# Layer 0's input rows added in its second loop, layer 2's outputs loaded into buffers of their own, and the v rows stored tile by tile

## The chip, the cores and the metric

The kernel runs on one core of a Trainium2 chip. The core has five engines with an instruction queue each: TensorE (PE, matrix products and transposes into the accumulation memory PSUM), VectorE (DVE), ScalarE (ACT), GpSimd (POOL) and SyncE (SP), which only issues DMAs. ScalarE and GpSimd issue DMAs as well, in the order of their own queues. Each queue is worked off in order, and an instruction waits in it for the semaphores of what it needs. The metric is the time on the device in microseconds (us), as the median of the timed runs; lower is better.

## The reference: four graph layers with residuals

The input x has 2708 rows of 512 features, and adj is a symmetric 2708 x 2708 matrix of zeros and ones. Each layer computes `x = layernorm(x + layer(x, adj))`. Cut to what matters here:

```python
# layer 0: the first 64 neighbours of each row
keep = Ab & (cumsum(Ab, axis=1) <= 64)
cnt  = keep.sum(axis=1)
xj = leaky_relu((keep @ x / max(cnt, 1)) @ W_nb.T + b_nb)
xi = leaky_relu(x @ W_line.T + b_line)
x  = layernorm(x + xi + where(cnt > 0, xj, 0))
# layer 1
agg = mask @ x / max(deg, 1)
x  = layernorm(x + relu(concat(x @ W_self + b_self, agg @ W_nb + b_nb) @ W_comb + b_comb))
# layer 2: attention with 8 heads of 64 features
e  = leaky_relu(f1[:, None] + f2[None, :], 0.2), masked by adj
x  = layernorm(x + softmax(e) @ Wh)
# layer 3: the same attention, elu, a second attention with one head, then an MLP 512-1024-512
x  = layernorm(x + MLP(elu(attention(elu(attention(x))))))
```

In layer 0 the layer norm therefore has three summands in each row: x itself, xi ("own rows"), and xj.

## The kernel before

Rows are handled in 22 tiles of 128 (the last has 20). What follows is only what the change touches; line numbers are those of the profile.

**Layer 0, first loop** (L297 to L324). For each tile TensorE transposes x and makes two products (L228): with W_nb (kept as a high and a low part, yH at L222 by ScalarE and yL at L223 by VectorE, which releases the accumulation tile), and with W_line. From the second product VectorE makes u = pm + b_line (L317), the leaky relu (`leaky`, L186) and adds the tile's x (L319); GpSimd stores u to `r0_dram` (L320). Between these, 14 of the tiles each have one block of rows of the adjacency mask prepared: ScalarE counts (L246), VectorE makes a running count in two halves (the scan L252 and the product L255), and TensorE transposes the mask (L264), which ScalarE writes to `maskT`. The second half of the running count is held behind the instruction named `low` on VectorE. Mask blocks are loaded by GpSimd (L241) into three buffers.

**Layer 0, second loop.** For blocks of up to four tiles TensorE accumulates the masked sums over all 22 column tiles (L460). The eight remaining mask blocks, the folding of layer 1's weights and the products for the attention vectors (L443, L444) go on beside it in small steps. When a block is summed, `finish` completes its tiles in steps that are taken one by one from the next block's loop: load r0, bias and leaky relu (L380, L186), a yield, then u * has + r0 (L383), the layer norm, and a store to `x1_dram`. The last block's steps fall into the loop that follows, layer 1's projection.

**Projections** (`project`, L568 to L681, called for layers 2, 3 and 4). For each tile: rows, transposed (L124, L126), 16 products (L627), small exponentials on ScalarE, and the scaled rows R2 (L656). Of each row's score b a factor v = exp(-0.8 b) is kept as a row (`keep_v`): TensorE transposes b (L604), ScalarE writes the exponential into `vrow` (L605), which is as wide as a block of the attention, and SyncE stores it to `v_dram` once for each block (L608). The attention loads v from there, spread over all partitions (L697, L712). For layers 2 and 3 the first such load is made at tile 14 (`first`).

**Layer 3's source** (`summed`, L929 to L938). A tile's attention output of layer 2 is loaded from `o_dram`, divided, x2 is added, and the layer norm is written over it; GpSimd stores it to `x3_dram` (L937), and TensorE transposes it. The tile comes from the ring "rows" of the pool `ahead`, three buffers, which r0, the rows of x and of x1 and others use too (`fetched`, L162 to L165). x2 comes into a ring of two buffers, "spare".

The order of the instructions in each queue is made by the framework's planner, from the order of the source, the dependences, the free buffers and its own estimates of durations. `issue_after` and `pe` add orders written by hand. A buffer is free again when the last instruction that uses its tile is done, a DMA included.

Of the kernel before, what the change touches and what calls it, by code (L numbers as in the profile page):

```python
# [9 lines left out]
F32 = mybir.dt.float32  # L10
# [3 lines left out]
AF = mybir.ActivationFunctionType  # L14
# [4 lines left out]
P = 128  # L19
D = 512  # L20
KD = D // P
EPS = 1e-5
ALPHA = 0.2
# [7 lines left out]
def kernel(  # L31
# [9 lines left out]
    nc = tc.nc  # L41
# [8 lines left out]
    def rows(t):  # L50
        return min(P, N - t * P)
# [31 lines left out]
    r0_dram = dram.tile([N, D], F32, name="r0_dram")  # L83
    x1_dram = dram.tile([N, D], F32, name="x1_dram")
    z1_dram = dram.tile([N, D], F32, name="z1_dram")
    x2_dram = dram.tile([N, D], F32, name="x2_dram")
    x3_dram = dram.tile([N, D], F32, name="x3_dram")


    o_dram = dram.tile([N, D], F32, name="o_dram")  # L90
# [15 lines left out]
    def layer_norm(pool, y, n, dst, on_scalar=False):  # L106
        st = pool.tile([P, 6], F32, name="ln_st")
        nc.vector.bn_stats(st[:n], y)
        mv = pool.tile([P, 2], F32, name="ln_mv")
        nc.vector.bn_aggr(mv[:n], st[:n])  # L110
        rs = pool.tile([P, 1], F32, name="ln_rs")
        nc.vector.tensor_scalar(rs[:n], mv[:n, 1:2], EPS, None, op0=OP.add)
        nc.gpsimd.tensor_tensor(rs[:n], rs[:n], half[:n], OP.pow)
        if not on_scalar:
            nc.vector.tensor_scalar(dst, y, mv[:n, 0:1], rs[:n], op0=OP.subtract, op1=OP.mult)
            return
        nc.vector.scalar_tensor_tensor(mv[:n, 0:1], mv[:n, 0:1], -1.0, rs[:n], op0=OP.mult, op1=OP.mult)
        nc.scalar.activation(dst, y, AF.Identity, bias=mv[:n, 0:1], scale=rs[:n])
# [22 lines left out]
    ahead = fast.enter_context(tc.tile_pool(name="ahead", bufs=2))  # L141
# [4 lines left out]
    def weight():  # L146
        return weight_tile().rearrange("p k a c -> p (k a c)")[:, :KD * D].rearrange("p (k c) -> p k c", k=KD)
# [14 lines left out]
    def fetched(src, t, n, pool=ahead, name="rows", bufs=None):  # L162
        x_ = pool.tile([P, D], F32, name=name, bufs=bufs or (3 if pool is ahead else None))
        nc.sync.dma_start(x_[:n], src[t * P:t * P + n, :])
        return x_[:n]  # L165
# [19 lines left out]
    def leaky(dst, u):  # L185
        return nc.vector.scalar_tensor_tensor(dst, u, 0.01, u, op0=OP.mult, op1=OP.max)  # L186
# [7 lines left out]
    with ExitStack() as phase:  # L194
# [17 lines left out]
        sm = phase.enter_context(tc.tile_pool(name="l01", bufs=2))  # L212
# [22 lines left out]
        cuts = [(b, min(b + 4, NT)) for b in range(0, NT, 4)]  # L235
        cuts = cuts[-1:] + cuts[:-1]
# [35 lines left out]
        def rows_of(src):  # L272
            return early(2, NT, lambda t: fetched(src, t, rows(t)))

        with ExitStack() as ph:
            st = ph.enter_context(tc.tile_pool(name="l0a", bufs=1))
            wnT, wlT = weight(), weight2
            room = [maskT[:, G + k, :4 * D].bitcast(F32) for k in range(2 * KD)]

            xs = rows_of(x)
            xTs = early(0, NT, lambda t, order=as_it_comes: transposed(ahead, ps_tr, xs(t), rows(t), "xT", order))

            transpose_weight(room[:KD], ps_tr, wnT, l0_w_nb)
            lows = {}
            for t in range(2):
                xT = xTs(t, order=pe)
                lows[t] = keep_y(t, P, product(xT, P, wnT, 0, pe))
            transpose_weight(room[KD:], ps_tr, wlT, l0_w_line)  # L290
            b_line = bias(bcast(l0_b_line, D))
            masks = early(1, HERE, lambda i: load_mask(i, st.tile([P, N], BF16, name="m", bufs=3)))
            masks(0)
            nc.gpsimd.memset(maskT[:, NT - 1, :], 0.0)
            nc.gpsimd.memset(maskT[:, :, N:], 0.0)
            counted = turned = 0
            for t in range(NT):  # L297
                n = rows(t)
                if t > 1:
                    lows[t] = keep_y(t, n, product(xTs(t, order=pe), n, wnT, 0, pe))  # L300
                xT = xTs(t)
                if t + 1 < NT:
                    xTs(t + 1, order=pe)
                while turned < counted - (t + 1 < NT):
                    for _ in turn(turned, masks(turned), lambda: sums(BF16, (P, G, P)), pe):
                        pass
                    turned += 1
                now = counted < min(HERE, -(-(t - 1) * HERE // (NT - 5)))
                if now:
                    m, places = masks(counted), st.tile([P, N // 2], BF16, name="places", bufs=1)  # L310
                    with tc.issue_after(highs[t].ins):
                        count(counted, m)
                    with tc.issue_after(lows[t].ins):
                        place(counted, m, places, 0, 2)
                pm = product(xT, n, wlT, 1, pe)
                u = sm.tile([P, D], F32, name="u")
                nc.vector.tensor_add(u[:n], pm[:n], b_line[:n])  # L317
                leaky(u[:n], u[:n])
                low = nc.vector.tensor_add(u[:n], u[:n], xs(t))  # L319
                nc.gpsimd.dma_start(r0_dram[t * P:t * P + n, :], u[:n])  # L320
                if now:
                    with tc.issue_after(low.ins):
                        place(counted, m, places, 1, 2)
                    counted += 1  # L324
# [3 lines left out]
        with ExitStack() as ph:  # L328
# [47 lines left out]
            def finish(ts_, us):  # L376
                for t in ts_:
                    n, u = rows(t), us[t]
                    r0 = fetched(r0_dram, t, n)
                    nc.vector.tensor_add(u[:n], u[:n], b_nb[:n])  # L380
                    leaky(u[:n], u[:n])
                    yield
                    nc.vector.scalar_tensor_tensor(u[:n], u[:n], has[:n, t:t + 1], r0, op0=OP.mult, op1=OP.add)  # L383
                    layer_norm(sm, u[:n], n, u[:n])
                    nc.gpsimd.dma_start(x1_dram[t * P:t * P + n, :], u[:n])
                    yield
# [63 lines left out]
            for i, b in enumerate(cuts):  # L450
# [19 lines left out]
                for t in ts_:  # L470
                    n = rows(t)
# [7 lines left out]
            xs = rows_of(x1_dram)  # L479
            xTs = early(0, NT, lambda t: transposed(ahead, ps_tr, xs(t), rows(t), "xT"))  # L480
            for t in range(NT):
                n = rows(t)
# [6 lines left out]
                u = sm.tile([P, D], F32, name="u")  # L489
# [3 lines left out]
        with ExitStack() as ph:  # L493
            st = ph.enter_context(tc.tile_pool(name="l1b", bufs=2))
            for t in range(NT):
                n = rows(t)
# [11 lines left out]
                u = sm.tile([P, D], F32, name="u")  # L508
# [5 lines left out]
    late = fast.enter_context(tc.tile_pool(name="late", bufs=1))  # L514
# [51 lines left out]
    def project(name, source, layer, v_dram, cuts, turned=None, first=None):  # L566


        w_src, w_view, _, heads = atts[layer]
# [9 lines left out]
        with ExitStack() as ph:  # L579
            sm = ph.enter_context(tc.tile_pool(name=f"{name}_s", bufs=2))  # L580
# [3 lines left out]
                           for k in (("pv", "pmm") if first else ("pmm", "pv")))  # L584
            if not first:
                ps_v, ps_mm = ps_mm, ps_v
            width = max(z - a for a, z in cuts) * P
            xs = early(1, NT, lambda t: source(sm, t, rows(t)))
            xTs = early(0, NT, lambda t: transposed(ahead, ps_tr, xs(t), rows(t), "xT"))
            if turned:  # L590
# [1 line left out]
                cuts_ = [(t, t + 1) for t in range(3)] + [(t, min(t + 2, NT)) for t in range(3, NT, 2)]  # L592
                parts = early(2, len(cuts_), lambda i: ready[i] if i in ready else turned(sm, *cuts_[i]))
                xTs = lambda t: parts(t if t < 3 else (t - 3) // 2 + 3)[:, :, ((t - 3) % 2 if t > 2 else 0) * P:][:, :, :P]
            vrows, bs, scaled = {}, {}, {}

            def keep_v(t):
                n = rows(t)
                a, z = next(c for c in cuts if c[0] <= t < c[1])
                if t == a:  # L600
                    vrows[a] = sm.tile([heads, width], F32, name="vrow", bufs=1)
                vrow = vrows[a]
                ps = ps_v.tile([P, P], F32, name="ps_v")
                nc.tensor.transpose(ps[:heads, :n], bs[t][:n, :heads], ident[:n, :n])  # L604
                nc.scalar.activation(vrow[:, (t - a) * P:(t - a) * P + n], ps[:heads, :n], AF.Exp, scale=ALPHA - 1.0)  # L605
                if t == z - 1:
                    cols = slice(a * P, a * P + (z - 1 - a) * P + n)
                    nc.sync.dma_start(v_dram[:, cols], vrow[:, :cols.stop - cols.start])  # L608

            for t in range(NT):  # L610
                n = rows(t)
# [53 lines left out]
                a, z = next(c for c in cuts if c[0] <= t < c[1])  # L665
# [68 lines left out]
    cuts = [-((-NT * i) // nb) for i in range(nb + 1)]  # L734
# [193 lines left out]

    def summed(sm, t, n):  # L929

        o, x2 = fetched(o_dram, t, n), fetched(x2_dram, t, n, late, "spare", 2)
        b = next(i for i, (a, z) in enumerate(blocks) if a <= t < z)
        by_head = o.rearrange("p (h c) -> p h c", h=H)
        nc.vector.tensor_mul(by_head, by_head, rcs[:n, b, :, t - blocks[b][0], None].to_broadcast([n, H, HO]))
        nc.vector.tensor_add(o, o, x2)
        layer_norm(late, o, n, o, on_scalar=True)
        nc.gpsimd.dma_start(x3_dram[t * P:t * P + n, :], o)  # L937
        return o  # L938

    loads, ready = [], {}  # L940

# [157 lines left out]
    scaled = project("p4", None, 2, vd[2], quads, elu_turned)  # L1099
# [327 lines left out]
```

## Time and profile before

| what | us |
|---|---|
| median of 3 timed runs | 2994.57 |
| lowest and highest of them | 2991.03, 2997.17 |
| the profiled execution | 2990.11 |
| its span, first to last instruction | 2988.3 |

Stretches of the span, with the busy time of the engines in each:

| stretch, us | work | TensorE | VectorE | ScalarE |
|---|---|---|---|---|
| 0 to 216 | layer 0, first loop | 189.25 | 166.47 | 93.07 |
| 216 to 506 | layer 0, second loop | 281.98 | 171.69 | 143.17 |
| 506 to 665 | layer 1, projection | 156.98 | 66.80 | 23.83 |
| 665 to 885 | layer 1, neighbour sums | 220.00 | 64.47 | 62.53 |
| 885 to 977 | layer 2, projection | 90.48 | 37.35 | 42.88 |
| 977 to 1523 | layer 2, attention | 533.53 | 536.26 | 506.49 |
| 1523 to 1640 | layer 3, projection | 104.05 | 77.16 | 62.60 |
| 1640 to 2185 | layer 3, first attention | 528.02 | 536.47 | 500.49 |
| 2185 to 2268 | layer 3, second projection | 80.52 | 36.72 | 38.65 |
| 2268 to 2988 | second attention and MLP | 702.62 | 304.49 | 60.02 |

The stretches are cut where one kind of product ends and the next begins; neighbouring stages overlap a little. An engine is busy while an instruction runs on it; DMA issues and waits don't count. Products are pipelined, so that a busy TensorE is not one at its peak. TensorE's granted clock was 0.995 of full speed over the span. In the page's lists "L164 rows<-o_dram" means that line 164 writes the tile rows from the tensor o_dram; numbers at the end of names are left out, so that x1_dram, x2_dram and x3_dram all read x_dram.

### The profile page before, as it was taken

What the parts mean: (1) busy time and instruction counts of PE and PEld (TensorE: products, weight loads), DVE (VectorE), ACT (ScalarE), POOL (GpSimd) and SP (SyncE); (2) the same over time, 40 slices, a digit from 0 to 9 for tenths busy, and PEclk for the clock granted to TensorE, in tenths of its full rate; (3) what the DMA queues carried; (4) which work ended last, traced back from release to release, by engine and by line L of the source; (5) the groups of instructions that cost most, each with busy time, mean ns of one, the idle gap of its engine ahead of it and who ended that gap; (6) DMA issues with size and microseconds to landing.
All of it is one profiled execution on the core that took longest, in us unless ns stands there. A gap on an engine that the chain in (4) does not pass through costs nothing.

```text
span 2988.3 us, 36484 instructions
## 1 busy us (share of the span) xinstructions
PE 2887.4 (97%) x14456; PEld 1606.4 (54%) x14456; DVE 1997.9 (67%) x2405; ACT 1533.7 (51%) x1774; POOL 219.8 (7%) x341
## 2 busy tenths in 40 slices
PE   8899999999999999999998999999999999999998
PEld 4447766448888333444466333444475555555555
DVE  6976639413234999999976999999964535445242
ACT  3546533113224999999965899999951000000001
POOL 1110101201110000000022000000000000000000
PEclk9999999999999999999999999999999999999999
DMA  4532325312222011111144111111061000000000
GB/s 120 113 92 59 86 72 143 129 62 85 84 74 80 28 52 39 38 48 44 33 126 140 40 40 39 41 55 46 28 160 60 4 25 14 25 14 15 14 22 20
DMA packets 117426, 180.05 MB, mean 60 GB/s; under 512 B 41042, under 2 KB 65507, under 8 KB 117246
## 3 DMA queue, kind: packets, MB, share of 16 engines
q1 hardware_dynamic: 88974, 116.47, 13.3%
q0 software_dynamic: 18160, 57.39, 6.8%
q10 hardware_dynamic: 10112, 3.77, 0.5%
q8 instruction: 116, 1.90, 0.3%
q14 instruction: 64, 0.52, 0.1%
HBM read 147.55 MB, written 44.65 MB: 64 GB/s over the span
## 4 chain that ended last, share of the span: by engine, by line
PE 64%; DVE 21%; ACT 7%; issue 5%; DMA 3%; POOL 0%; SPq 0%; DVEq 0%; POOLq 0%; ACTq 0%
PE pn L1056 13%; PE po L895 13%; DVE e L703 12%; PE acc L506 7%; PE pm L228 7%; PE pm L627 5%; PE pl L1031 5%; PE pl L1022 5%; ACT c L730 4%; PE acc L460 4%; DVE places L252 2%; PE pd L799 2%; PE ps_tr L124 1%; DMA rows<-o_dram 1%; DVE maskT L485 1%
## 5 line engine op out<-in xcount | busy, mean ns | idle before, releaser
L703 DVE SCALAR_TENSOR_TENSOR e<-v_bc,ucol,maskT 128x1408 f32<-128x1408 f32 (+3 forms) x804 | 1135.6, 1469 | 324.4 <-PE pn L1056 314.3
L730 ACT ACTIVATE c<-e,bcol 128x1300 fp8e4<-128x1300 f32 (+1 forms) x688 | 967.7, 1423 | 75.0 <-DVE e L703 30.0
L895 PE MATMUL po<-e,R 128*64 128x512 f32 (+2 forms) x4224 | 903.8, 547 | 30.2 <-DVE e L703 27.2
L895 PEld LDWEIGHTS po<-e,R 128*64 128x64 f32 x4224 | 338.7, 136 | 562.3 <-issue 396.6
L1056 PE MATMUL pn<-e,R 128*128 128x512 f32 (+1 forms) x1056 | 413.4, 542 | 0.0
L1056 PEld LDWEIGHTS pn<-e,R 128*128 128x128 f32 x1056 | 191.0, 190 | 199.3 <-issue 196.1
L1024 ACT ACTIVATE w<-pl,b 128x256 f32<-128x256 f32 (+1 forms) x88 | 40.9, 465 | 372.9 <-PE pl L1022 364.8
L460 PE MATMUL acc<-yH,kT 128*128 128x512 f32 x484 | 197.3, 408 | 5.0 <-ACT kT L335 5.0
L228 PE MATMUL pm<-w,xT 128*128 128x512 f32 (+1 forms) x384 | 177.7, 606 | 22.1 <-DVE yL L223 18.7
L460 PE MATMUL acc<-yL,kT 128*128 128x512 f32 x484 | 189.3, 391 | 0.0
L506 PE MATMUL acc<-yH,mf 128*128 128x512 f32 x484 | 188.4, 389 | 0.0
L506 PE MATMUL acc<-yL,mf 128*128 128x512 f32 x484 | 188.3, 389 | 0.0
L627 PE MATMUL pm<-w,xT 128*128 128x264 f32 (+1 forms) x704 | 171.1, 398 | 3.6 <-DVE R L656 2.2
L228 PE MATMUL pm<-weight,xT 128*128 128x512 f32 (+1 forms) x352 | 160.2, 598 | 2.3 <-DVE u L317 1.5
L1031 PE MATMUL pl<-lin,w 128*128 128x512 f32 (+1 forms) x352 | 157.4, 592 | 0.0
L1022 PE MATMUL pl<-lin 128*128 128x256 f32 (+1 forms) x704 | 153.4, 371 | 3.7 <-DVE lin L924 3.7
L627 PEld LDWEIGHTS pm<-w,xT 128*128 128x128 f32 (+1 forms) x704 | 131.9, 193 | 30.3 <-ACT xT L126 3.0
L1022 PEld LDWEIGHTS pl<-lin 128*128 128x128 f32 x704 | 129.1, 190 | 34.4 <-issue 15.8
L503 ACT CAST mf<-maskT 128x1024 fp32r<-128x1024 fp8e4 (+1 forms) x66 | 64.4, 977 | 158.0 <-PE acc L506 147.9
L222 ACT CAST yH<-pm 128x512 fp32r<-128x512 f32 (+1 forms) x44 | 25.7, 585 | 229.3 <-PE pm L228 229.3
L335 ACT ACTIVATE kT<-maskT 128x512 fp32r<-128x512 fp8e4 (+1 forms) x132 | 77.5, 594 | 116.6 <-PE acc L460 116.6
L228 PEld LDWEIGHTS pm<-w,xT 128*128 128x128 f32 (+1 forms) x384 | 70.8, 189 | 120.4 <-issue 99.2
(215 smaller groups left out, 2713.1 us busy)
## 6 DMA issues: line engine op xcount, KB each, us to landing
rows<-x_dram SPq DMA_DIRECT2D x63, 256.0 KB
v_bc<-v_dram SPq DMA_DIRECT2D x16, 704.0 KB
x_dram<-u POOLq DMA_DIRECT2D x42, 256.0 KB, 2.4
v_bc<-v_dram SPq DMA_DIRECT2D x16, 650.0 KB
m<-in_adj_dram POOLq DMA_DIRECT2D x13, 677.0 KB, 8.5
rows<-in_x_dram SPq DMA_DIRECT2D x21, 256.0 KB
r_dram<-u POOLq DMA_DIRECT2D x21, 256.0 KB, 3.3
rows<-r_dram SPq DMA_DIRECT2D x21, 256.0 KB
```

Source lines behind the costliest of these rows:

```text
L228: order(nc.tensor.matmul(pm[:n], xT[:, k, :n], w[:, k, :], start=(k == 0), stop=(k == KD - 1)))
L335: made = nc.scalar.activation(kT[:, :w], maskT[:, j, b[0] * P:b[0] * P + w], AF.Relu, scale=-1.0)
L460: nc.tensor.matmul(pa[t], kT[:, (t - b[0]) * P:(t - b[0] + 1) * P], y[:, j, :], start=(j == 0 and y is yH), stop=(j == NT - 1 and y is yL))
L503: nc.scalar.copy(mf[:, :g1 - g0, :], maskT[:, g0:g1, t * P:(t + 1) * P])
L506: nc.tensor.matmul(pa, mf[:, j - g0, :], y[:, j, :], start=(j == 0 and y is yH), stop=(j == NT - 1 and y is yL))
L627: nc.tensor.matmul(pm[a][:m, :D // 2 + heads], xT[:, k, :m], w[:, k, a, :D // 2 + heads], start=(k == 0), stop=(k == KD - 1))
L703: self.made = nc.vector.scalar_tensor_tensor(e[:, :w], v[:, :w], ucol[:, j, h:h + 1], maskT[:, j, c0:c0 + w], op0=OP.max, op1=OP.mult)
L730: nc.scalar.activation(c[:, :w], e[:, :w], AF.Sigmoid, bias=bcol[:, j, h:h + 1], scale=STEP, saturate=False)
L895: pe(nc.tensor.matmul(po[i][HO * k:HO * k + HO, :c1 - c0], R2[:, j, h * HO:(h + 1) * HO], e[:, c0:c1], start=(i_ == 0), stop=(i_ == NT - 1)))
L1022: nc.tensor.matmul(pl[:, :w], self.lin1[:, k, f * P:(f + 1) * P], h[:, k, :w], start=(k == 0), stop=(k == KD - 1))
L1031: nc.tensor.matmul(pl[:n], gT[:, f, (t - t0) * P:(t - t0) * P + n], self.lin2[:, f, :], start=(f == 0), stop=(f == KF - 1))
L1056: nc.tensor.matmul(pn[k][:, :w], R2[:, j, k * P:(k + 1) * P], e[:, :w], start=(j == 0), stop=(j == NT - 1))
```

## The change

Three parts, put in together.

1. In layer 0's first loop the add of the tile's x is taken out, and `low` is now the leaky relu. In `finish` a second tile is loaded beside r0, the tile of x, and is added to r0 in the same step, ahead of the yield.
2. In `project`, `vrow` is one tile wide (with the pool's two buffers in place of one), and each tile's v is stored at once, from ScalarE's queue.
3. In `summed`, tiles from the third on are loaded into a ring "o" of three buffers in the projection's own pool, and the layer norm writes into a tile of "rows". The first two tiles stay as they were.

```diff
@@ -315,8 +315,7 @@
                 pm = product(xT, n, wlT, 1, pe)
                 u = sm.tile([P, D], F32, name="u")
                 nc.vector.tensor_add(u[:n], pm[:n], b_line[:n])
-                leaky(u[:n], u[:n])
-                low = nc.vector.tensor_add(u[:n], u[:n], xs(t))
+                low = leaky(u[:n], u[:n])
                 nc.gpsimd.dma_start(r0_dram[t * P:t * P + n, :], u[:n])
                 if now:
                     with tc.issue_after(low.ins):
@@ -376,9 +375,10 @@
             def finish(ts_, us):
                 for t in ts_:
                     n, u = rows(t), us[t]
-                    r0 = fetched(r0_dram, t, n)
+                    r0, x0 = fetched(r0_dram, t, n), fetched(x, t, n)
                     nc.vector.tensor_add(u[:n], u[:n], b_nb[:n])
                     leaky(u[:n], u[:n])
+                    nc.vector.tensor_add(r0, r0, x0)
                     yield
                     nc.vector.scalar_tensor_tensor(u[:n], u[:n], has[:n, t:t + 1], r0, op0=OP.mult, op1=OP.add)
                     layer_norm(sm, u[:n], n, u[:n])
@@ -584,7 +584,6 @@
                            for k in (("pv", "pmm") if first else ("pmm", "pv")))
             if not first:
                 ps_v, ps_mm = ps_mm, ps_v
-            width = max(z - a for a, z in cuts) * P
             xs = early(1, NT, lambda t: source(sm, t, rows(t)))
             xTs = early(0, NT, lambda t: transposed(ahead, ps_tr, xs(t), rows(t), "xT"))
             if turned:
@@ -592,20 +591,15 @@
                 cuts_ = [(t, t + 1) for t in range(3)] + [(t, min(t + 2, NT)) for t in range(3, NT, 2)]
                 parts = early(2, len(cuts_), lambda i: ready[i] if i in ready else turned(sm, *cuts_[i]))
                 xTs = lambda t: parts(t if t < 3 else (t - 3) // 2 + 3)[:, :, ((t - 3) % 2 if t > 2 else 0) * P:][:, :, :P]
-            vrows, bs, scaled = {}, {}, {}
+            bs, scaled = {}, {}
 
             def keep_v(t):
                 n = rows(t)
-                a, z = next(c for c in cuts if c[0] <= t < c[1])
-                if t == a:
-                    vrows[a] = sm.tile([heads, width], F32, name="vrow", bufs=1)
-                vrow = vrows[a]
+                vrow = sm.tile([heads, P], F32, name="vrow")
                 ps = ps_v.tile([P, P], F32, name="ps_v")
                 nc.tensor.transpose(ps[:heads, :n], bs[t][:n, :heads], ident[:n, :n])
-                nc.scalar.activation(vrow[:, (t - a) * P:(t - a) * P + n], ps[:heads, :n], AF.Exp, scale=ALPHA - 1.0)
-                if t == z - 1:
-                    cols = slice(a * P, a * P + (z - 1 - a) * P + n)
-                    nc.sync.dma_start(v_dram[:, cols], vrow[:, :cols.stop - cols.start])
+                nc.scalar.activation(vrow[:, :n], ps[:heads, :n], AF.Exp, scale=ALPHA - 1.0)
+                nc.scalar.dma_start(v_dram[:, t * P:t * P + n], vrow[:, :n])
 
             for t in range(NT):
                 n = rows(t)
@@ -928,14 +922,17 @@
 
     def summed(sm, t, n):
 
-        o, x2 = fetched(o_dram, t, n), fetched(x2_dram, t, n, late, "spare", 2)
+
+        o = fetched(o_dram, t, n) if t < 2 else fetched(o_dram, t, n, sm, "o", 3)
+        x2 = fetched(x2_dram, t, n, late, "spare", 2)
         b = next(i for i, (a, z) in enumerate(blocks) if a <= t < z)
         by_head = o.rearrange("p (h c) -> p h c", h=H)
         nc.vector.tensor_mul(by_head, by_head, rcs[:n, b, :, t - blocks[b][0], None].to_broadcast([n, H, HO]))
         nc.vector.tensor_add(o, o, x2)
-        layer_norm(late, o, n, o, on_scalar=True)
-        nc.gpsimd.dma_start(x3_dram[t * P:t * P + n, :], o)
-        return o
+        x3 = o if t < 2 else ahead.tile([P, D], F32, name="rows", bufs=3)[:n]
+        layer_norm(late, o, n, x3, on_scalar=True)
+        nc.gpsimd.dma_start(x3_dram[t * P:t * P + n, :], x3)
+        return x3
 
     loads, ready = [], {}
 
```

## The prediction

> **What bounds the kernel now.** I read the page's engine shares first (TensorE busy 97% of the span), then busy time by stretch, then in each touched stretch the waits and the timeline. The average hides that TensorE is not the limit everywhere. The change touches four stretches: layer 0's first loop (36 to 216 us), layer 0's second loop with the start of layer 1's projection (216 to 552), and the projections of layers 2 (885 to 977) and 3 (1523 to 1640).
>
> In the first loop VectorE sets the pace. One tile of it on VectorE's timeline (start, length, engine, line, operation):
>
> ```profile
> 117.53 0.66 DVE L223 TENSOR_TENSOR yL<-pm,yH 128x512 fp32r<-128x512 f32 x1
> 118.11 0.85 DVE L255 TENSOR_TENSOR m<-m,places 128x1354 bf16<-128x1354 bf16 x1
> 119.07 2.98 DVE L252 TENSOR_TENSOR_SCAN places<-m,over 128x1354 bf16<-128x1354 bf16 x1
> 122.08 0.87 DVE L255 TENSOR_TENSOR m<-m,places 128x1354 bf16<-128x1354 bf16 x1
> 122.87 0.68 DVE L317 TENSOR_TENSOR u<-pm,bias 128x512 f32<-128x512 f32 x1
> 123.58 0.69 DVE L186 SCALAR_TENSOR_TENSOR u<-u 128x512 f32<-128x512 f32 x1
> 124.31 0.69 DVE L319 TENSOR_TENSOR u<-u,rows 128x512 f32<-128x512 f32 x1
> 124.92 3.03 DVE L252 TENSOR_TENSOR_SCAN places<-m,places,over 128x1354 bf16<-128x1354 bf16 x1
> 127.87 0.66 DVE L223 TENSOR_TENSOR yL<-pm,yH 128x512 fp32r<-128x512 f32 x1
> ```
>
> From one yL (L223) to the next is 10.34 us without a gap. TensorE has less: 16 products at 0.43, four transposes (0.44 together) and 22 mask transposes (1.43 together), 8.8 us; its largest wait from 20 to 214 us says whom it waits for:
>
> ```profile
> PE pm L228 <- DVE yL L223: 15.7, 13, 2.0
> ```
>
> In layer 3's projection the same products as in layer 2's take longer. Sixteen tiles of each (columns: stretch, length, then busy us and instruction count of PE, PEld, DVE, ACT, POOL; clock; DMA share; GB/s):
>
> ```profile
> 893.20:958.90 65.70, 65.70 (x337) 55.77 (x336) 22.40 (x82) 23.64 (x83) 3.70 (x16) 1.00 0.32 95
> 1537.80:1615.90 78.10, 71.03 (x338) 56.45 (x336) 56.21 (x181) 33.62 (x99) 24.29 (x49) 0.98 0.61 190
> ```
>
> Layer 2 runs at TensorE's 4.11 us a tile, layer 3 at 4.88. The chain of waits and SyncE's own waits from 1525 to 1660 us name the reason: the load of a tile's attention output stands behind the store of an earlier tile, since both use one of three "rows" buffers.
>
> ```profile
> 1599.05 3.90 DMA x_dram<-rows
> 1603.03 5.15 DMA rows<-o_dram
> ```
> ```profile
> SPq L164 <- DMA x_dram<-rows: 34.4, 12, 6.7
> ```
>
> In the second loop TensorE is the limit, but at its end VectorE is full as well:
>
> ```profile
> 490.00:533.00 43.00, 41.01 (x134) 22.62 (x132) 42.08 (x58) 10.31 (x18) 6.42 (x5) 1.00 0.62 171
> ```
>
> **Part 1, taken away in the first loop.** One VectorE add (L319) a tile goes. 14 of the 22 tiles carry a mask scan and stand on VectorE's chain; the others run at TensorE's pace or wait for ScalarE's count, and lose nothing. 14 x 0.70 (0.69 and its gap) = 9.8 us. What is late next: VectorE then needs 9.64 a tile, TensorE 8.8, ScalarE about 6.8, so VectorE stays the bound and all of it shows. The mask loads are close: the load behind the store of r0 on POOL's queue was issued at 105.17 and its count began at 114.18, ending 2.2 us before the scan that needs it. Over three tiles (three mask buffers) the shorter period takes 2.1 us, and the store's wait ending an add earlier returns 0.7. So about 0.8 us of slack remains, with landings between 6.1 and 12.4 us (median 8.2). I give up one tile's gain: **-9**, between -9.8 and -3.
>
> **Part 2, added in the second loop.** Each tile gets a 256 KB load of x on SyncE's queue and an add r0 += x0 (0.6 to 0.69 us, the row L319) on VectorE, 22 x 0.65 = 14 us of VectorE and 5.5 MB of reads. Until about 470 us VectorE is busy 28 to 30 of every 45 us, so four adds a block are covered by TensorE's accumulation. From 470 to 552 us nothing covers them: VectorE is busy 98%, and in it fall the ends of about eight tiles. TensorE waits there 2.0 us for yL and would wait longer: at most 8 x 0.65 = 5.2 us. The mask comparisons (L485, 22 x 1.5 us), which are due only in the next stage, can give way to part of that. I take +2.5.
>
> The add is also a new wait: it stands before the step's yield, so it needs x0 and r0 one step earlier than r0 was needed. Behind it on VectorE are yL (which releases TensorE's pm) and the mask scans. The buffer that x0 takes is free when the tile before has used its r0 (L383). The load needs some 3 us (r0's neighbours in the chain: 2.7 to 3.2), while VectorE has bn_stats, the scale (L115), the bias add and the leaky relu first, over 3 us with the wait for POOL's power. So it arrives in time when the loop goes at its pace; I put no more on it. Ends: 0 and +33 (rival 3). On SyncE later loads stand behind x0's buffer wait; the x1 rows of the projection need one buffer per 7.3 us, and a load of 3 us fits.
>
> **Part 3, the o ring in layer 3.** No arithmetic changes. Loads need a buffer that ScalarE's L118 has read, not one whose store has landed. Load 0 issued at 1563.47; L934 began at 1567.54; L118 ended at 1572.42; the store went out at 1572.71 and load 3 at 1576.83. That is 13.36 us for three tiles, and 4.4 of it goes: some 9.0 for three, far under TensorE's 12.3. A second coupling: SyncE issues x2, x2, o, o in pairs, so that o waits behind x2's buffer (L935). With o's buffer free sooner the planner can put o first, as the source does. What is late next is VectorE: busy 56.2 us in the sixteen tiles, and 9.5 more waiting for POOL's power, 65.7, exactly TensorE's 65.7. With two engines so even some waits will stay: 4.25 us a tile, between TensorE's 4.11 and the old 4.88. 16 x 0.63 = **-10**. Ends: 0 (the pairing stays) and -12.4 with another -5.4 (the last six tiles, 22.8 us against layer 2's 17.4, where ScalarE's table loads of 1.28 us also stand; I leave those).
>
> **Part 4, v stored tile by tile.** 66 stores in place of 10, on ScalarE's queue instead of SyncE's. Issue rows: SyncE's v store 0.27 us median, a ScalarE store 0.33:
>
> ```profile
> 2188.46 0.33 ACTq L855 DMA_DIRECT2D rc_dram<-spare  x1
> ```
>
> With the wait for the vrow just written I count 0.43. [...] v is first read at tile 14, three tiles (12 us) after tile 10's store, and a vrow buffer is needed again two tiles (8.2 us) later. I go by the row: 22 x 0.43 = 9.5 us of ScalarE per projection, covered by TensorE where ScalarE is busy 43 of 92 us (layer 2). It isn't covered in the last six tiles, where ScalarE is busy 15.5 of 17.4 (layer 2) and 20.5 of 22.8 (layer 3): six stores, 2.6 us, exceed the gaps of 1.9 and 2.3 by 0.7 and 0.3. **+1**; ends 0 and +19 for all 44 on the path. That SyncE no longer waits for vrow (20.2 and 14.1 us in its waits) gives nothing: TensorE waits for no load in layer 2's projection. Layer 4's six stores becoming 22 cost nothing by the same cover.
>
> **Sum.** -9 + 2.5 - 10 + 1 = -15.5 us. The profiled execution took 2990.1 (span 2988.3), so 2974.6 for such a one. Its time lies 4.5 below the median of the three timed runs, 2994.6; against that median: **2979**.
>
> **Rivals.**
> 1. The o ring brings little: the x2, x2, o, o pairing stays or VectorE's order keeps the 9.9 us pair. For it: SyncE's order in the trace, and VectorE's zero margin. Against: o is fetched before x2 in the source, and layer 3's first four tiles ran at 4.11. Then -9 - 1 + 2.5 + 1: 2988.
> 2. Mask loads take over in the first loop: -3 instead of -9, 2985. For it: the slack of 0.8 us; against: the median landing.
> 3. Slower: VectorE stands at the new add from 470 to 552 us waiting for x0, since three buffers now serve x1, r0 and x0 and SyncE issues in order. For it: L383 already waited 2.0 us for an r0 there. Price: eight tiles x (0.65 + 3.8, the median from an o load's issue to landing), less 3 of slack, +33 instead of +2.5: 3009. Against: before 550 us no r0 came late. It decides from 1.9 us of wait a tile (8 x 2.6 - 3 = 18, what parts 1, 3 and 4 give).
> 4. The planner makes another order and the gains are lost elsewhere, so that the change does not do what it says: 2995.
>
> **Chances.** Forecast 0.62 (its own range 2971 to 2987), rivals 0.16, 0.07, 0.09, 0.06. The range takes in rivals 1 and 2 and the lower end of part 3: 2968 to 2994. Faster by over 0.2% means under 2988.6: most of the forecast, half of rival 1, rival 2: 0.77. Within 0.2%, about what a measurement of this kernel can tell from no change: 0.12. Slower: 0.11.
>
> **What would show it.** Part 1: yL to yL near 9.65 us at 118 us, the first loop over by about 207. Part 2: VectorE's waits for loads of x at the new add, TensorE's waits for yL between 470 and 552 under 6 us. Part 3: no SyncE wait for the x3 store, sixteen tiles in about 68 us. Part 4: ScalarE's queue shows stores of 0.33 us, TensorE waits for vrow no longer than 1.4. I am wrong if the gap between v transposes in layer 3 stays near 4.9 us, or the second loop grows by over 8 us.

## The result and the profile after

| | us |
|---|---|
| changed kernel, median of 10 runs (lowest to highest) | 2981.47 (2976.48 to 2988.02) |
| kernel before, median of 10 runs beside them | 2993.85 (2991.03 to 2998.87) |
| ratio, 95% interval | 0.9959, 0.9949 to 0.9968 |
| profiled execution of the changed kernel; its span | 2981.41; 2979.5 |

12.4 us are gone, where the forecast had 15.5 taken off. The two profiled executions differ by 8.7 only, because the one of the changed kernel happened to start late: its first yL came at 18.91 us (before: 15.74), and one group of eight products ahead of its third yL took 5.40 us instead of 3.70, at a granted clock of 0.69. The same kernel profiled again started at 15.66, and a third time at 17.76, and had no such group ahead of that yL. So I cut the spans at events on TensorE, VectorE and ScalarE and compare pieces. Here are before, the changed kernel's first profile and two further ones of it (us; "sums" is ScalarE's copy of a finished block's sums, L473; "v" the transpose of a tile's scores, L604 before and L600 after):

| piece | before | changed | again | again |
|---|---|---|---|---|
| first yL to last yL (first loop) | 200.90 | 195.18 | 193.49 | 193.49 |
| last yL to first copy of sums | 30.49 | 33.85 | 35.05 | 36.11 |
| first to last block's copy of sums | 251.58 | 248.47 | 248.63 | 248.71 |
| to the last v of layer 2 | 477.56 | 478.17 | 478.31 | 478.79 |
| to the first po of layer 2's attention | 0.70 | 5.16 | 5.16 | 5.15 |
| to the first v of layer 3 | 560.86 | 559.51 | 558.19 | 560.96 |
| first v to first po of layer 3 | 102.63 | 91.89 | 91.27 | 91.23 |
| to the first pn | 627.64 | 628.15 | 629.33 | 628.77 |
| to the end | 720.20 | 720.21 | 720.71 | 720.43 |

Here po and pn are the products of the attentions with eight heads (L889, before L895) and with one.

Two pieces became shorter as forecast, one that nobody had priced became shorter by 3, and two became longer.

**First loop.** VectorE's timeline of the changed kernel, one tile from yL to yL:

```profile
119.76 0.68 DVE L223 TENSOR_TENSOR yL<-pm,yH 128x512 fp32r<-128x512 f32 x1
...
124.14 0.68 DVE L317 TENSOR_TENSOR u<-pm,bias 128x512 f32<-128x512 f32 x1
124.86 0.69 DVE L186 SCALAR_TENSOR_TENSOR u<-u 128x512 f32<-128x512 f32 x1
125.47 3.03 DVE L252 TENSOR_TENSOR_SCAN places<-m,places,over 128x1354 bf16<-128x1354 bf16 x1
...
129.31 0.68 DVE L223 TENSOR_TENSOR yL<-pm,yH 128x512 fp32r<-128x512 f32 x1
```

The second scan follows the leaky relu directly: 9.55 us instead of 10.34.

**Start of the second loop.** The same kernel, VectorE's timeline (in brackets the idle time before an instruction and what ended it):

```profile
214.09 0.68 DVE L223 TENSOR_TENSOR yL<-pm,yH 20x512 fp32r<-20x512 f32 x1 [2.80 <-ACT yH L222]
221.70 0.69 DVE L381 TENSOR_TENSOR rows<-rows 128x512 f32<-128x512 f32 x1 [6.93 <-DMA rows<-in_x_dram]
222.31 0.67 DVE L317 TENSOR_TENSOR u<-pm,bias 20x512 f32<-20x512 f32 x1
```

then ScalarE's and TensorE's:

```profile
216.53 0.70 ACT L334 ACTIVATE kT<-maskT 128x256 fp32r<-128x256 fp8e4 x2
223.01 0.35 ACTq L216 DMA_DIRECT2D bias<-in_L_gnn_b_nb_dram  x1
223.46 0.72 ACT L334 ACTIVATE kT<-maskT 128x256 fp32r<-128x256 fp8e4 x2 [6.23 <-DVE u L317]
```
```profile
223.93 0.50 PE L460 MATMUL acc<-yH,kT 128*128 128x512 f32 x1 [3.62 <-ACT kT L334]
```

Read them from the top. The new add r0 += x0 of tile 20, which needs no sums, was put ahead of L317 of the last tile on VectorE, and waited 6.93 us there for x. L317 is the last reader of the one "bias" buffer. The load of b_nb into that buffer stands on ScalarE's queue; it waited, and the mask copies kT behind it waited too. TensorE stood 3.62 us. Before, its longest wait in this piece was one of 2.10 us, some microseconds later:

```profile
229.56 0.51 PE L460 MATMUL acc<-yH,kT 128*128 128x512 f32 x1 [2.10 <-ACT kT L335]
```

**Start of layer 2's attention.** ScalarE and TensorE of the changed kernel:

```profile
974.89 0.27 ACT L601 ACTIVATE vrow<-ps_v 8x128 f32<-8x128 f32 x1
...
975.27 1.28 ACT L724 ACT_TABLE_LOAD   x1
976.57 1.47 ACT L724 ACTIVATE c<-e,bcol 128x1408 fp8e4<-128x1408 f32 x1
978.05 1.28 ACT L634 ACT_TABLE_LOAD   x1
...
979.52 0.16 ACT L601 ACTIVATE vrow<-ps_v 8x20 f32<-8x20 f32 x1
```
```profile
979.74 2.69 PE L889 MATMUL po<-e,R 128*64 128x512 f32 x6 [4.78 <-ACT vrow L601]
```

The last two v's were transposed together at 974.58, but the last vrow stands behind a c (L724, an activation of the attention) with a table load of 1.28 us before and after it, and po waits for that vrow. Before, no c stood in between:

```profile
976.97 8.67 PE L895 MATMUL po<-e,R 128*64 128x512 f32 x40 [0.31 <-ACT vrow L605]
```

**Layer 3's projection.** Sixteen tiles (columns as in the forecast), and SyncE's waits from 1525 to 1660 us:

```profile
1539.20:1611.10 71.90, 67.58 (x338) 55.57 (x337) 56.99 (x191) 35.20 (x97) 26.19 (x52) 1.00 0.68 219
```
```profile
SPq L164 <- ACT rows L118: 21.5, 11, 3.3
```

The wait for the store of x3 (34.4 us, 12 times) is no longer in the list; loads now wait for L118, the reader. 71.9 us instead of 78.1.

### The profile page after: what moved, and what is told of

Same layout as the page of the kernel before. It is cut to its first block, busy times and chain, and to the rows that moved or that the text cites. A ratio compares the mean times of both kernels' runs of the same rounds, so it can differ in the third digit from the quotient of the medians.

```text
span 2979.5 us, 36582 instructions
## 1 busy us (share of the span) xinstructions
PE 2882.4 (97%) x14456; PEld 1603.3 (54%) x14456; DVE 1995.1 (67%) x2405; ACT 1534.6 (52%) x1772; POOL 214.9 (7%) x341
## 4 chain that ended last, share of the span: by engine, by line
PE 64%; DVE 20%; ACT 7%; issue 5%; DMA 3%; POOL 0%; SPq 0%; ACTq 0%; DVEq 0%; POOLq 0%
PE pn L1053 13%; PE po L889 13%; DVE e L697 12%; PE acc L506 7%; PE pm L228 6%; PE acc L460 6%; PE pl L1028 5%; PE pm L621 5%; ACT c L724 5%; PE pl L1019 5%; PE pd L793 2%; DVE places L252 2%; PE ps_tr L124 1%; DMA o<-o_dram 1%; DVE maskT L485 1%
## 5 line engine op out<-in xcount | busy, mean ns | idle before, releaser
L724 ACT ACTIVATE c<-e,bcol 128x1300 fp8e4<-128x1300 f32 (+1 forms) x688 | 968.0, 1423 | 76.9 <-DVE e L697 33.0
L889 PE MATMUL po<-e,R 128*64 128x512 f32 (+2 forms) x4224 | 905.7, 548 | 33.1 <-DVE e L697 25.5
L889 PEld LDWEIGHTS po<-e,R 128*64 128x64 f32 x4224 | 339.2, 137 | 566.7 <-issue 398.1
L113 POOL TENSOR_TENSOR ln_rs<-ln_rs,half 128x1 f32<-128x1 f32 x88 | 57.9, 658 | 1473.0 <-DVE ln_rs L112 1404.5
L1019 PEld LDWEIGHTS pl<-lin 128*128 128x128 f32 x704 | 129.1, 190 | 34.4 <-issue 15.8
L621 PEld LDWEIGHTS pm<-w,xT 128*128 128x128 f32 (+1 forms) x704 | 128.0, 187 | 29.6 <-ACT xT L126 4.1
```

The lines of the kernel that those rows point to most:

```text
L621: nc.tensor.matmul(pm[a][:m, :D // 2 + heads], xT[:, k, :m], w[:, k, a, :D // 2 + heads], start=(k == 0), stop=(k == KD - 1))
L724: nc.scalar.activation(c[:, :w], e[:, :w], AF.Sigmoid, bias=bcol[:, j, h:h + 1], scale=STEP, saturate=False)
L889: pe(nc.tensor.matmul(po[i][HO * k:HO * k + HO, :c1 - c0], R2[:, j, h * HO:(h + 1) * HO], e[:, c0:c1], start=(i_ == 0), stop=(i_ == NT - 1)))
L1019: nc.tensor.matmul(pl[:, :w], self.lin1[:, k, f * P:(f + 1) * P], h[:, k, :w], start=(k == 0), stop=(k == KD - 1))
```

## The experiments

**The parts alone.** Three kernels on the kernel before: the first loop's add moved to `finish` (parts 1 and 2); the v stores (part 4); the v stores and the o ring (parts 3 and 4; the o ring needs the room that the wide vrow gives up). With them ran the changed kernel.

> Only part 1 and part 2 of the change: x is added in the second loop's finish instead of the first loop; v stores and loads of o as before. My reading of the two traces: the first loop is 7.4 us shorter from tile 2's yL to tile 17's, the first block of the second loop stands some 3.4 us (VectorE at the add of x for tile 20, ahead of the last tile's L317), 2.7 us of which come back later in the loop; together -6 us against before (ratio 0.998). The first po of layer 2's attention starts 2.4 us after the last v transpose, as before. Prediction's own terms: -9 and +2.5, -6.5. Rival (the move is worth nothing because the second loop gives all of it back): 0, ratio 1.000.

> Only part 4: v stored tile by tile on ScalarE's queue, two vrow buffers; first loop and loads of o as before. Trace reading (a ring of two vrows): the last vrow of layer 2 stands behind a c on ScalarE, the first po waits for it 4 to 5 us, about 1.4 us of it come back by layer 3: +3 to +5 us against before, nearly all of it between the last v transpose of layer 2's projection and the first po. Prediction's term (issue time of 66 small DMAs): +1 spread over the three projections. Layer 3's first projection keeps its gaps of some 4.9 us from v transpose to v transpose.

> Parts 3 and 4: v stores tile by tile and the o ring; first loop as before. The difference to the run with the v stores alone is the o ring's worth. Theory: layer 3's first projection is 10 to 11 us shorter from its first v transpose to the first po of its attention, whole run -6 to -8 us against before (o ring -10.7, stores +3 to +5). Rival 1 of the prediction (the ring brings little, the x2,x2,o,o pairing stays): -2 from the ring, whole run +1 to +3.

> The changed kernel itself, on the same chip as its parts: -12 us against before (ratio 0.996). If the parts are independent, the run with parts 1 and 2 and the run with parts 3 and 4 add to it within 2 us. It also shows whether the two slow product groups at 12 and 27 us of the changed kernel's trace (6.4 and 5.4 us against 3.7) come again: if they belong to the clock and not to the change, they are as short as before or stand elsewhere.

| kernel | median, us (runs) | ratio to before, 95% |
|---|---|---|
| parts 1, 2 | 2989.30 (21) | 0.9987, 0.998 to 0.9993 |
| part 4 | 2994.66 (13) | 1.0003, 0.9993 to 1.0013 |
| parts 3, 4 | 2986.03 (16) | 0.9975, 0.9967 to 0.9983 |
| all | 2981.89 (7) | 0.9955, 0.9939 to 0.9971 |

The parts add up: 0.0013 + 0.0025 = 0.0038 of the time against 0.0045 and, in the first comparison, 0.0041. Parts 1 and 2 bring 3.9 us (2.1 to 6.0), a little less than the 6 expected. The first po comes 0.69 us after the last v without the v stores (before: 0.70; the 2.4 of the expectation was a misreading) and 5.16 us with them, so that this gap belongs to part 4. Yet part 4 costs 0.9 us as a whole (-2.1 to 3.9) and not 3 to 5. Layer 3 shows why. Rows of before (its sixteen tiles stand in the forecast), of part 4 alone and of parts 3 and 4, each cut at the seventeenth v and at the first po:

```profile
1615.90:1640.40 24.50, 20.16 (x83) 14.52 (x81) 14.35 (x38) 22.18 (x41) 6.83 (x11) 0.86 0.09 33
```
```profile
1543.60:1621.70 78.10, 70.27 (x339) 56.58 (x337) 55.97 (x183) 35.06 (x100) 25.10 (x49) 0.98 0.61 191
1621.70:1641.80 20.10, 17.00 (x83) 12.29 (x80) 13.80 (x37) 18.27 (x38) 6.04 (x11) 1.00 0.19 59
```
```profile
1542.00:1613.30 71.30, 67.85 (x338) 55.46 (x337) 56.95 (x191) 34.95 (x97) 26.59 (x52) 1.00 0.70 221
1613.30:1633.40 20.10, 16.93 (x83) 12.46 (x81) 12.38 (x30) 18.94 (x42) 2.16 (x8) 1.00 0.05 11
```

The o ring takes 6.8 us off the sixteen tiles and nothing off the rest. The v stores take nothing off the sixteen tiles and 4.4 off the last six, where the clock (the figure after the counts) was 0.86 before and 1.00 with them. Part 4 gains here what it loses in layer 2. TensorE's timelines of the last six tiles, before and with part 4 alone, show where:

```profile
1627.16 0.27 PE L604 MATMUL ps_v<-ident,b 128*8 128x128 f32 x1 [2.07 <-DVE b L634]
...
1628.40 10.38 PE L627 MATMUL pm<-w,xT 128*128 128x264 f32 x32
```
```profile
1631.32 7.52 PE L621 MATMUL pm<-w,xT 128*128 128x264 f32 x32
```

The wait for VectorE's b is gone, and the 32 products of the last two tiles take 7.52 us instead of 10.38; the granted clock in these 10.38 us was 0.72 (0.50 up to 1634 us, 0.98 from there on). The two other profiles with wide rows (parts 1 and 2, and the kernel that follows) have the same wait, 2.06 us, and 9.2 us for these products.

**Which half of the v stores does that?** The kernel before with its ten wide stores on ScalarE's queue:

```diff
-                    nc.sync.dma_start(v_dram[:, cols], vrow[:, :cols.stop - cols.start])
+                    nc.scalar.dma_start(v_dram[:, cols], vrow[:, :cols.stop - cols.start])
```

> The kernel before with its ten wide v stores on ScalarE's queue instead of SyncE's, the wide vrow kept. It parts the two halves of the v-store edit. In the run with narrow stores layer 3's last six tiles took 20.1 us from tile 16's v transpose to the first po, before 24.6. If SyncE's queue being free of the v store gives that: 20 to 21 us here too. If the narrow rows give it: 24 us or more. In layer 2 the first po should come within 1 us of the last v transpose, since the wide row has no ring to wait for. Whole run -4 to +1 against before.

The last six tiles took 24.1 us and the first po of layer 2 came after 0.70: the change of queue alone gives neither, so both need the narrow rows. The ratio, 0.9986 (0.998 to 0.9993), was better than I expected of a mere change of queue. No piece of its profile owns these 4 us. Its layer 0, which the edit doesn't touch, took 31.98 and 249.89 in the pieces where before has 30.49 and 251.58; and with parts 1 and 2 alone the sixteen tiles of layer 3, which these don't touch, took 81.7 instead of 78.1. So one profile doesn't resolve a piece to better than 1.5 us, in places not to better than 3.6.

**The ring of two vrows.** Four vrow buffers in layer 2's projection; and, in another kernel, the small stores on SyncE's queue with two buffers:

```diff
-                vrow = sm.tile([heads, P], F32, name="vrow")
+                vrow = sm.tile([heads, P], F32, name="vrow", bufs=4 if layer == 0 else None)
```
```diff
-                nc.scalar.dma_start(v_dram[:, t * P:t * P + n], vrow[:, :n])
+                nc.sync.dma_start(v_dram[:, t * P:t * P + n], vrow[:, :n])
```

> The changed kernel with four vrow buffers instead of two in layer 2's projection (two in the others). Theory (the first po of layer 2's attention comes 5.16 us after the last v transpose because the last vrow waits for a store to give a buffer back and so stands behind a c with two table loads): 5.16 becomes under 1 us, as it was before the change (0.70), whole run -3 to -4.5 us against the changed kernel, ratio to before 0.9945. Rival (the small DMAs' own issue time on ScalarE, 0.27 us each): the 5.16 us stay above 4, run unchanged.

> The changed kernel with the 66 v stores on SyncE's queue instead of ScalarE's, vrow buffers as they are (two). If the issue of the stores on ScalarE is what the stores cost, ScalarE is freed of 66 issues and layer 2's projection ends without the 5.16 us; if the ring of two vrows sets it, the last vrow still stands behind a c and the 5.16 us stay above 4. Whole run within 2 us of the changed kernel either way, unless SyncE's loads for layer 3's projection stand behind v stores: then that stretch (91 us) grows by some us.

With four buffers the gap ahead of po fell from 5.16 to 0.79 us; with the stores on SyncE it stayed at 5.10. So the ring sets it, and not the stores' issue on ScalarE: these two runs leave the rival out. In the time the first repair alone doesn't show: 2980.39 us, 0.9953 (0.994 to 0.9966), against 0.9955 for the changed kernel, though the profiled span was 2970.6. Part of the gain comes back in layer 2's attention, 561.35 us to layer 3's first v where the changed kernel had 558.19 to 560.96. On SyncE the stores were worse, 0.9968 (0.9956 to 0.9979): layer 3's piece took 95.89 us instead of 91.2 to 91.9. Its last six tiles took 18.5 us up to the last v, as in the changed kernel (18.4; before 23.1), but then the first po came after 4.90 us instead of 1.69. So the narrow rows speed up these tiles on either queue, and SyncE's queue gives 3.2 us of it back at their end. Whether that is the ring again (a c stands ahead of the last vrow) or a load of v behind the stores, which the profile names, isn't settled.

**The early add.** One kernel adds x behind the sums, so that the add can't be put ahead; another leaves the add where it is and cuts the chain at the load of b_nb, which goes to GpSimd's queue:

```diff
-                    nc.vector.tensor_add(r0, r0, x0)
                     yield
                     nc.vector.scalar_tensor_tensor(u[:n], u[:n], has[:n, t:t + 1], r0, op0=OP.mult, op1=OP.add)
+                    nc.vector.tensor_add(u[:n], u[:n], x0)
```
```diff
-        def bias(src):
+        def bias(src, queue=nc.scalar):
             b = sm.tile([P, D], F32, name="bias", bufs=1)
-            nc.scalar.dma_start(b, src)
+            queue.dma_start(b, src)
...
-            b_nb = bias(bcast(l0_b_nb, D))
+            b_nb = bias(bcast(l0_b_nb, D), nc.gpsimd)
```

> The changed kernel with x added to u after has*u + r0 instead of to r0 ahead of it, so that the add needs the sums and can't be put ahead of the last tile's L317 on VectorE. Theory: VectorE's 6.8 us wait for x ahead of L317 goes, and with it ScalarE's 6.1 us before kT and TensorE's 3.5 and 1.0 to 1.7 us at the start of the second loop: from tile 21's yL to ScalarE's first copy of the sums 30.5 us as before the change, where the changed kernel has 33.9 and 35.1; whole run -3.4 to -4.6 against the changed kernel. Rival (the wait moves on: the last r0 store, or the load of x, is what all wait for): 33 us or more, run unchanged.

> The changed kernel with the load of b_nb (L216, waits for the one bias buffer, which the last tile's L317 reads) on GpSimd's queue instead of ScalarE's. VectorE's early wait for x stays. Theory (chain: x's load, VectorE's early add, L317 of tile 21, bias load on ScalarE's queue, kT behind it, TensorE): cut at the bias load, kT is no longer late, and TensorE's 3.5 us stall at the start of the second loop goes though VectorE still waits 6 to 7 us: tile 21's yL to first copy of the sums 30 to 31.5 us, whole run -2.5 to -4.6 against the changed kernel. Rival (VectorE's wait itself is what TensorE meets): the stall stays.

In both, TensorE's stall at the fifth pair of products is gone, so the chain is the one told above: VectorE's wait does no harm by itself. But I expected 30.5 us for the piece, and they took 32.88 and 32.40. A second wait, 2.10 us long in the kernel before, now stands first. ScalarE's and TensorE's timelines of the kernel with the load on GpSimd:

```profile
224.44 2.55 ACT L246 ACTIVATE spare<-spare,gate 128x2708 bf16<-128x2708 bf16 x1 [0.87 <-DMA spare<-in_adj_dram]
```
```profile
227.44 0.50 PE L460 MATMUL acc<-yH,kT 128*128 128x512 f32 x1 [2.51 <-ACT kT L334]
```

ScalarE's count of the next mask waits for the mask's load, and kT stands behind the count. So of the 3.4 to 5.6 us only a part was to be had: both kernels stood here longer than the 2.10 us of before (3.07 with the add behind the sums, 2.51 with the load on GpSimd), and in both some products after the wait were slow (0.43 us apart instead of 0.23). The ratios are 0.9954 (0.9942 to 0.9967) and 0.9943 (0.993 to 0.9956). The first shows no gain; its time from the last copy of sums to layer 2's first product was 389.42 us, 387.3 to 388.0 in the changed kernel. The second is better by 0.0012 than the changed kernel beside the parts, which the intervals don't part.

**The masks in the first loop.** The store of r0 on SyncE's queue, so that no mask load stands behind it:

```diff
-                nc.gpsimd.dma_start(r0_dram[t * P:t * P + n, :], u[:n])
+                nc.sync.dma_start(r0_dram[t * P:t * P + n, :], u[:n])
```

> The changed kernel with the stores of r0 on SyncE's queue, so that the mask loads on GpSimd's queue no longer stand behind a store that waits for VectorE's leaky. Theory (rival 2 of the prediction in part: in the tiles after a turn without a mask, the scan waits for a mask that was loaded late, 10.6 us instead of 9.55): these tiles come down toward 9.55, first loop -2 to -4 us against the changed kernel. Other outcomes: the mask's buffer and not the queue holds the load back, no change of those tiles; or SyncE's queue, where the loads of x now stand behind the stores, makes the first loop longer.

No tile changed by more than 0.01 us. The mask loads' own waits in this kernel say why the loads don't come earlier; GpSimd's timeline:

```profile
75.53 0.71 POOL L241 DMA_DIRECT2D m<-in_adj_dram  x1 [10.57 <-PE acc L264]
```

The load waits for the transposes that read the buffer's last mask. A fourth mask buffer wasn't tried. But the theory was wrong at its root: the scans didn't wait for late masks. In two of the three profiles of the changed kernel no count of ScalarE waits for a mask load, in the third one does, for 1.38 us, and no tile is longer for it; the 10.6 us have another reason (part 1 below). Ratio 0.9955 (0.9943 to 0.9967).

**Both repairs together.** Four vrow buffers in layer 2 and b_nb on GpSimd's queue, beside the changed kernel once more:

> The changed kernel once more, beside the two kernels below on the same chip: ratio to before 0.9955 to 0.996.

> The changed kernel with both repairs: four vrow buffers in layer 2's projection, and the load of b_nb on GpSimd's queue. If the two are independent and their gains in the profiles count in the time (5.16 to 0.79 us ahead of the first po, of which 1.5 to 2.5 come back in layer 2's attention; and about 1.5 to 2.6 us at the start of the second loop): -3 to -5 us against the changed kernel, ratio to before 0.994 to 0.9945. If the first po's wait is hidden later: -1 to -2.5.

The changed kernel took 2982.55 us, 0.9954 (0.9941 to 0.9968); with both repairs 2972.81 us (2970.04 to 2976.64), 0.9927 (0.9913 to 0.9941). That is 9.7 us less (8.1 by the ratios), more than the 3 to 5 expected, and the best kernel here. The two repairs alone, beside the changed kernel of an earlier comparison, were worth 0.0002 and 0.0012 of the time, 4 us together; why the pair brings more isn't shown. In the profiles the piece at the start of the second loop fell from 36.11 to 31.73 and the one ahead of po from 5.15 to 0.80; 1.5 came back in layer 2's attention. These are 7.2, of which some 2.7 are slow products in the changed kernel's profile (last section); the profiled kernel also started 2.0 earlier, which is none of the repairs' doing. TensorE's timeline of it at the two places:

```profile
222.31 0.51 PE L460 MATMUL acc<-yH,kT 128*128 128x512 f32 x1 [2.18 <-ACT kT L334]
...
968.62 8.16 PE L889 MATMUL po<-e,R 128*64 128x512 f32 x38 [0.41 <-ACT vrow L601]
```

## Why the forecast was right, point by point

It was 2979 and the kernel took 2981.5, so the sum held. Of its terms, parts 1 and 3 had the right mechanism and were too large by 1.6 and 3.2 us; parts 2 and 4 came near their totals because costs and gains that I hadn't seen cancelled.

**Part 1, -9: measured -7.4.** Mechanism right, term too large, and not through rival 2. Eight tiles lost 0.72 to 0.78 each, as counted, and two lost 1.1 and 1.7. But four tiles became longer by 0.2 to 0.6: each of these holds three of VectorE's products L255 (0.86 us) where it held two. Before, the last product of each run of tiles with a mask came behind the next yL and so fell into the tile without a mask that follows; now it comes ahead of that yL. VectorE's timelines at such a place, before and changed (profiled again):

```profile
90.16 0.66 DVE L223 TENSOR_TENSOR yL<-pm,yH 128x512 fp32r<-128x512 f32 x1
90.74 0.85 DVE L255 TENSOR_TENSOR m<-m,places 128x1354 bf16<-128x1354 bf16 x1
```
```profile
87.05 0.86 DVE L255 TENSOR_TENSOR m<-m,places 128x1354 bf16<-128x1354 bf16 x1
87.83 0.69 DVE L223 TENSOR_TENSOR yL<-pm,yH 128x512 fp32r<-128x512 f32 x1
```

The tile without a mask has room for the product: it took 5.14 us with it and 5.16 without, and VectorE then waited 1.65 and 3.15 us for yH. The tiles with a mask have none. There are three such runs, so that 3 x 0.86 = 2.6 us are to be taken from 14 x 0.75 = 10.5; a new wait of 0.53 us of one scan for a mask copy of ScalarE (L268) leaves about 7.4. The step that was too much is "all of it shows": VectorE stayed the bound, but it was given other work in the place of the adds. Rival 2 took nothing. The scans' waits for ScalarE's count at the start of each run (3.76, 2.66 and 2.34 us) are as long before as after.

**Part 2, +2.5: measured +0.9 to +4.0 over the three profiles, for other reasons.** The step put the price at 470 to 552 us, where VectorE is full. There TensorE's waits for yL were 1.7 us after and 2.0 before (all its waits 3.2 and 2.7): the adds cost next to nothing there. Rival 3's wait, VectorE standing at the new add for x, did come, with 6.93 us and not at its forecast place: "four adds a block are covered" left out that the first block's adds have no block before them and may be placed in front of the first loop's last tile. That cost 3.4 to 5.6 us. (The longest wait at the new add, 40.2 us at 446.91, cost nothing: before, VectorE stood 47.4 us at this place with no work.) And about 3 us were gained where I looked for none, as TensorE's timelines show, before and after:

```profile
400.97 5.37 PE L228 MATMUL pm<-w,xT 128*128 128x512 f32 x8 [1.95 <-DMA w<-in_L_gnn_W_comb_dram]
```
```profile
400.34 3.67 PE L228 MATMUL pm<-w,xT 128*128 128x512 f32 x8 [0.85 <-ACT kT L334]
```

With the loads of x among them, SyncE's loads stood in another order: W_comb was issued at 394.23, ahead of two W_self loads that stood ahead of it before (395.17). In this profile TensorE no longer waits for it; in the two others of the changed kernel it waits 1.25 and 1.20 us. So the order gives 0.7 to 1.1 us. The other 1.7 are the eight products, which ran at a granted clock of 1.00 (before: 0.68); that part isn't shown to be the order's doing, since with the wide stores on ScalarE, where layer 0 is that of before, they took 3.67 us too after the same wait of 1.95. I had asked of each moved load what stands behind it, and not what it lets pass.

**Part 3, -10: measured -6.8 in the sixteen tiles.** The coupling through the store is gone as told, and VectorE is what TensorE waits for most, as told: 3.0 of its 4.1 us of waits from 1538 to 1603 us in the first profile. But the tile came to 4.46 us and not 4.25. "Some waits will stay" was the right sentence with too small a number. VectorE's lack of margin also has another cause than the one told: its waits for POOL's power fell from 9.1 to 0.8 us in this stretch, and those for loads of o rose from 5.4 to 8.1. Rival 1 is out.

**Part 4, +1: measured +4.5 at layer 2's end and -4.4 in layer 3's last six tiles, 0.9 in all.** I priced 0.43 us of ScalarE for each store, and the right total came out of two things that I hadn't seen. "A vrow buffer is needed again two tiles later" holds in the steady tiles; at the end three v's come within 4.1 us, and a planner that finds no free vrow puts a c with its two table loads (1.28 us each) in between. In layer 3's last six tiles the narrow rows take away a wait of 2.07 us and let 32 products run 2.9 us faster; why the order that comes with narrow rows has no such wait isn't settled. Nor is it settled that a SyncE queue free of v stores "gives nothing": the wide stores on ScalarE's queue gave 4.2 us (2.1 to 6.0), which no piece owns. 56 more stores cost 0.9 us in all (-2.1 to 3.9), and in layer 2 the issue of one took 0.27 us of ScalarE's queue. A store counted in one place, where the ring of two made the next vrow stand back: po came 5.16 us after the last v, and 0.79 us after it with four buffers.

**The sum.** -7.4, about +2.4, -6.8 and about 0 make -11.8, against 12.4 measured; the forecast's -15.5 was too much by the terms of parts 1 and 3. That parts 2 and 4 came out near their terms was luck.

## What to carry to other kernels

Before pricing an added instruction by its neighbours, ask how early it may be placed: one that needs only a load can be put in front of work that others wait for. After taking one away from a full engine, count that engine's work per tile again: something else may have moved into its place. Keep a load that must wait for a buffer off the queue of an engine with work behind it, and let the ring of a buffer with an asynchronous store hold as many tiles as come together at the stage's end, not as many as in its steady part. A repair of one wait shows the next: count with what stands second, and allow for slow products after a pause of TensorE (here 1.6 and 2.7 us after stalls of 3.55 and 3.47, and none after 3.62 and 3.48).

## What the hardware showed

**Products can be slow after a pause of TensorE.** In one profile of the changed kernel the stall of 3.55 us at the second loop's start was followed, 1.3 us later, by products 0.43 us apart instead of 0.23. TensorE's timeline:

```profile
218.91 0.50 PE L460 MATMUL acc<-yH,kT 128*128 128x512 f32 x1 [3.55 <-ACT kT L334]
...
220.91 0.63 PE L460 MATMUL acc<-yL,kT 128*128 128x512 f32 x1
221.33 0.63 PE L460 MATMUL acc<-yH,kT 128*128 128x512 f32 x1
...
223.81 0.40 PE L460 MATMUL acc<-yH,kT 128*128 128x512 f32 x1
```

Eight products lost 0.2 us each, 1.6 us, in a slow stretch of 3.3 us. In the third profile thirteen products after a stall of 3.47 us were 0.43 us apart, some 2.7 us lost in a stretch of 5.7 us; in the first none was slow, after 3.62 us. This is most of why one piece, the start of the second loop, took 33.85, 35.05 and 36.11 us in three profiles of one kernel. Slow products followed a shorter wait too: in the kernel before, those after 1.95 us of waiting for W_comb took 5.37 us, 1.7 too long, at a granted clock of 0.68 (0.50 from 403 to 405 us). Nor is it certain: after the same wait in the kernel with wide stores on ScalarE's queue, and after 3.48 us at the start of the second loop in the kernel with four vrow buffers, nothing slowed. What decides it isn't shown.

**A load beside two mask loads.** The 256 KB of x issued at 214.40 beside two mask loads of 677 KB let the add begin at 221.70, 7.3 us later, where I had taken some 3 us from quieter places. In those 7.3 us the DMA engines were busy for 0.96 of the time, at 210 GB/s.
